# Loading a sample in pieces of eight lines instead of four, in a subject-indexed matrix product with a residual

## The chip, the cores and the metric

The kernel runs on one NeuronCore of a Trainium2 chip; the other cores are idle. The metric is the device time of one execution in microseconds. Before the change it is 326.57 us, the median of three runs (326.31 to 326.69). One further execution was recorded by the hardware profiler; the profile's times are of that one.

## The reference

```python
# x: (128, 128, 1024) float32, subjects: (128,) int32 in 0..7, weights: (8, 128, 128) float32
w = weights[subjects]
out = x + jnp.einsum('bct,bcd->bdt', x, w)
```

For each of 128 samples a 128x128 matrix is chosen by the sample's subject, the sample (128 lines of 1,024 numbers, 512 KB) is multiplied by it, and the sample itself is added. 64 MiB are read and 64 MiB are written.

## The kernel before

All of the weights are loaded once into SBUF (`w_all`). The samples go through SBUF in tiles of four samples (`H * G`, 2 MB): tile `i` lives in slot `i % SLOTS` of twelve buffers `x0` to `x11`, with line `c` of a sample on partition `c`. There are 32 tiles (`NT`). The program is unrolled and its order is written by hand, with one stream of instructions for each engine and semaphores between them.

- SP issues the load of the weights and then all loads of `x`, one DMA for each sample (`load`, called from the loop at line 162). From the thirteenth tile on it first waits until the slot's earlier tile has been stored (lines 165 and 167).
- For each pair of samples (64 of them), POOL waits for the pair's loads and copies the two chosen matrices out of `w_all` (line 196); the index is a register that was loaded from the subjects.
- PE multiplies: four matmuls of 512 columns for a pair's two samples (line 206), into one of two PSUM buffers.
- DVE adds PSUM to the sample and writes the sum over the sample in its slot (line 217).
- ACT issues the store of a tile from the same slot when both pairs are done (`store`, line 223); the first and the last tile are stored in smaller parts.

SP's and ACT's transfers run on two queues over the same 16 DMA engines. A DMA's semaphore rises by one for each of the 16 engines that has finished its share.

`transfer` (line 50) builds the DMA instruction from the two access patterns that it is given. `load` hands it the sample in DRAM regrouped: `ROWS` lines that follow each other in DRAM become one row of the source pattern, and the destination pattern remains 128 partitions of 4 KB each. With `ROWS = 4` the source of a sample is 32 rows of 16 KB, and each goes to four neighbouring partitions. Stores do not use `ROWS`: each partition's 8 KB for two samples is one piece on the SBUF side.

Of the kernel before, what the change touches and what calls it, by code (L numbers as in the profile page):

```python
# [42 lines left out]

IDLE = 3

ROWS = 4
QUEUES = {mybir.EngineType.SP: "qSPDynamicHW", mybir.EngineType.Activation: "qActDynamicHW"}


# [21 lines left out]
def kernel(  # L71
# [49 lines left out]
    def load(engine, i, q):  # L121
# [4 lines left out]
            xs[k][:, q, :],  # L126
            x[i * H * G + q].rearrange("(a r) t -> a (r t)", r=ROWS),
        ).then_inc(s_pair[k][h], DMA)
# [137 lines left out]
```

## Time and profile before

| what | value |
|---|---|
| median of three runs | 326.57 us |
| the profiled execution: its own time | 327.18 us |
| the profiled execution: span from the first to the last instruction | 325.4 us |
| PE busy | 241.1 us (74%) |
| DVE busy | 147.9 us (45%) |
| POOL busy | 34.3 us (11%) |
| read from and written to HBM | 67.63 MB and 67.11 MB |
| mean rate over the span | 414 GB/s |
| loads of `x`: issue to landing, median of 128 | 32.3 us |
| stores of four samples: issue to landing, median of 30 | 47.3 us |
| last load of `x` lands | 271.4 us after the start of the span |

The profile cuts the span into 40 slices and gives for each the busy share of every engine in tenths, the mean busy share of the 16 DMA engines, and the bytes per second. A row for a stretch of time (a window) gives its length, the busy time of PE, of PE's weight loads, of DVE and of POOL with the number of instructions in brackets, the granted TensorE clock, the DMA share and GB/s. A row of waits reads: who waited, at which line, for what; microseconds in total, number of waits, the longest. A queue's row gives its packets, its megabytes and the time of its packets as a share of 16 engines' span.

### The profile page before, as it was taken

How to read it: one execution, taken by the hardware profiler on the slowest of the kernel's cores; microseconds unless marked ns; L12 is line 12 of the kernel's file. 1: busy time of each engine (PE TensorE's matmuls, PEld its weight loads, DVE VectorE, ACT ScalarE, POOL GpSimd, SP SyncE). 2: the span in 40 equal slices, each digit the busy share in tenths (PEclk: the TensorE clock that was granted, in tenths of full speed). 3: DMA queues.
4: the chain of work that ended last, by engine and by line, in shares of the span. 5: the costliest groups of instructions: out<-in, count | busy, mean ns of one | idle time of the engine just before them, and what ended most of it. 6: DMA issues, size and time to landing. Idle time of an engine off the chain costs nothing.

```text
span 325.4 us, 1606 instructions
## 1 busy us (share of the span) xinstructions
PE 241.1 (74%) x518; PEld 95.2 (29%) x518; DVE 147.9 (45%) x68; POOL 34.3 (11%) x132
## 2 busy tenths in 40 slices
PE   6999988988888888888888888888888689000000
PEld 2444332333333333333333333333333233000000
DVE  1375754555555555454555555554554544200000
POOL 1011111011111111111011111111111010000000
PEclk9999999999999999999999999999999889655555
DMA  6999999999999999999999999999999999999994
GB/s 250 413 418 421 428 425 422 420 428 427 426 421 427 429 415 427 424 431 423 423 435 417 416 432 424 428 417 428 433 419 424 418 437 415 429 425 427 426 428 201
DMA packets 16074, 134.85 MB, mean 414 GB/s; under 512 B 2625, under 2 KB 3650, under 8 KB 3906
## 3 DMA queue, kind: packets, MB, share of 16 engines
q1 hardware_dynamic: 7184, 67.64, 49.7%
q10 hardware_dynamic: 8882, 67.11, 49.1%
q8 instruction: 4, 0.07, 0.1%
q14 instruction: 4, 0.03, 0.0%
HBM read 67.63 MB, written 67.11 MB: 414 GB/s over the span
## 4 chain that ended last, share of the span: by engine, by line
PE 42%; DVE 20%; issue 16%; POOL 4%; DMA 2%; POOLq 1%; SPq 0%
PE ps L206 42%; DVE x L217 20%; POOL w L196 4%; DMA x<-in_x_dram 2%; POOLq L196 1%; SPq L57 0%; SPq L161 0%; POOLq L139 0%; SPq L262 0%; SPq L139 0%
## 5 line engine op out<-in xcount | busy, mean ns | idle before, releaser
L206 PE MATMUL ps<-x,w 128*128 128x512 f32 x512 | 236.1, 607 | 33.6 <-POOL w L196 32.1
L217 DVE TENSOR_TENSOR x<-ps,x 128x2048 f32<-128x2048 f32 x64 | 146.7, 2292 | 129.1 <-PE ps L206 129.1
L206 PEld LDWEIGHTS ps<-x,w 128*128 128x128 f32 x512 | 93.3, 191 | 176.6 <-issue 93.9
L196 POOL COPY w<-w_all 128x128 f32 x128 | 34.1, 296 | 238.0 <-DMA x<-in_x_dram 207.7
L146 PE MATMUL ps<-zeros 128*128 128x512 f32 x6 | 5.0, 992 | 1.7 <-DVE zeros L143 1.7
L146 PEld LDWEIGHTS ps<-zeros 128*128 128x128 f32 x6 | 1.8, 328 | 3.7 <-issue 2.1
L143 DVE MEMSET zeros<- 128x512 f32 x1 | 0.5, 485 | 1.1 <-SPq L139 1.1
L153 DVE TENSOR_SCALAR near<-given 1x128 int32<-1x128 int32 x1 | 0.2, 215 | 0.6 <-DMA given<-in_itok_B_dram 0.6
L157 DVE CUSTOM_DVE_ANT_0 index<-near,wrap 1x256 uint16<-1x256 uint16 x1 | 0.3, 278 | 0.0
L155 DVE TENSOR_SCALAR wrap<-near 1x128 int32<-1x128 int32 x1 | 0.2, 216 | 0.0
L253 POOL MEMSET const-float32-0.0<- 128x1 f32 x1 | 0.1, 99 | 0.2 <-issue 0.2
L253 POOL MEMSET const-bfloat16-1.0<- 128x1 bf16 x1 | 0.1, 102 | 0.0
L253 POOL MEMSET const-uint8-127<- 128x1 uint8 x1 | 0.1, 102 | 0.0
L253 POOL MEMSET const-float32-1.0<- 128x1 f32 x1 | 0.1, 99 | 0.0
## 6 DMA issues: line engine op xcount, KB each, us to landing
x<-in_x_dram SPq DMA_DIRECT2D x128, 512.0 KB, 32.3
out_dram<-x ACTq DMA_DIRECT2D x30, 2048.0 KB, 47.3
out_dram<-x ACTq DMA_DIRECT2D x3, 1024.0 KB, 13.9
out_dram<-x ACTq DMA_DIRECT2D x2, 512.0 KB, 21.1
w_all<-in_L_cond_weights_dram SPq DMA_DIRECT2D x1, 512.0 KB, 4.5
given<-in_itok_B_dram ACTq DMA_DIRECT2D x1, 0.5 KB
```

Of the source, the lines that this page charges most:

```text
L143: nc.vector.memset(zeros, 0.0).then_inc(s_zeros, 1)
L146: nc.tensor.matmul(ps[P_SLOTS - 1][:, G - 1, :N], zeros[:, :D], zeros, start=True, stop=True)
L153: nc.vector.tensor_scalar(near, given, -S, S - 1, ALU.max, ALU.min).then_inc(s_index, 1)
L155: nc.vector.tensor_scalar(wrap, near, 0, S, ALU.is_lt, ALU.mult).then_inc(s_index, 1)
L157: nc.vector.tensor_tensor(index, near, wrap, ALU.add).then_inc(s_index, 1)
L196: copy = nc.gpsimd.tensor_copy(ws[b % W_SLOTS], w_all[:, bass.ds(subject[b % R], 1), :])
L206: mm = nc.tensor.matmul(p[:, q % G, t : t + N], ws[(i * H * G + q) % W_SLOTS][:, 0, :], xs[k][:, q, t : t + N], start=True, stop=True,)
L217: nc.vector.tensor_tensor(mine, p, mine, ALU.add).then_inc(s_added, 1)
L253: nc = _bacc.Bacc("TRN2", target_bir_lowering=False, num_devices=1)
```

## The change

One constant is changed. A sample's source pattern becomes 16 rows of 32 KB, and each goes to eight neighbouring partitions; the destination pattern, the number of DMAs, their order, and everything else remain.

```diff
-ROWS = 4
+ROWS = 8
```

It is used in one place:

```python
    def load(engine, i, q):
        k, h = i % SLOTS, q // G
        transfer(
            nc,
            engine,
            xs[k][:, q, :],
            x[i * H * G + q].rearrange("(a r) t -> a (r t)", r=ROWS),
        ).then_inc(s_pair[k][h], DMA)
```

## The prediction

> **What bounds the kernel now.** I began with the slices of the page: a kernel is bound by whatever row never dips.
>
> ```profile
> PE   6999988988888888888888888888888689000000
> DVE  1375754555555555454555555554554544200000
> DMA  6999999999999999999999999999999999999994
> GB/s 250 413 418 421 428 425 422 420 428 427 426 421 427 429 415 427 424 431 423 423 435 417 416 432 424 428 417 428 433 419 424 418 437 415 429 425 427 426 428 201
> ```
>
> The reader is to see that the DMA row is full from the second slice to the last but one, and that the bytes per second stay the same when PE and DVE have nothing left to do (the last five slices). So the transfers set the end, not arithmetic. The queues say how the time of the 16 DMA engines is divided:
>
> ```profile
> DMA packets 16074, 134.85 MB, mean 414 GB/s; under 512 B 2625, under 2 KB 3650, under 8 KB 3906
> ...
> q1 hardware_dynamic: 7184, 67.64, 49.7%
> q10 hardware_dynamic: 8882, 67.11, 49.1%
> ```
>
> q1 is SP's queue (loads), q10 is ACT's (stores); each takes half of the engines' time. Third, the stretches:
>
> ```profile
> 10.00:14.00 4.00, 4.00 (x11) 1.85 (x10) 2.09 (x1) 0.00 (x0) 1.00 1.02 414
> 60.00:100.00 40.00, 34.90 (x76) 13.43 (x75) 21.99 (x10) 5.34 (x20) 1.00 1.01 425
> 276.00:300.00 24.00, 0.35 (x1) 0.00 (x0) 2.29 (x1) 0.00 (x0) 0.56 1.01 427
> 322.00:325.40 3.40, 0.00 (x0) 0.00 (x0) 0.00 (x0) 0.00 (x0) 0.50 0.04 14
> ```
>
> The last column is GB/s: 414 with loads alone, 425 with loads and stores mixed, 427 with stores alone. The waits show what stands behind whom:
>
> ```profile
> POOL w L196 <- DMA x<-in_x_dram: 207.7, 55, 5.6
> DVE x L217 <- PE ps L206: 129.1, 64, 9.0
> ...
> SPq L57 <- DMA out_dram<-x: 78.5, 10, 9.8
> ```
>
> Computation waits for loads (first row), and SP for slots that the stores must empty (last row, in the SP queue's own answer). The DMA engines have work through all of it, so neither wait is on the path.
>
> **The sum of before.** The trace also holds one record for each packet: size, start, duration. A load of one sample is 32 packets of 16 KB (4,096 in all), two for each engine, and 16 four-byte packets that raise the semaphore. A 16 KB load packet lasts 616 ns at the 10th, the 50th and the 90th percentile once stores run, and the next packet of its engine starts 613 ns after it; an 8 KB store packet lasts 311 and is followed after 307; a 4 KB one lasts 159 and is followed after 155. Per engine: 256 load packets by 613 = 156.9 us; 504 stores by 307 = 154.7; 16 short ones by 155 = 2.5; 64 pieces of the weights by 24 ns = 1.5; 164 semaphore packets by 5.5 ns = 0.9. Sum 316.5. The first weights move at 2.1 us and most engines end at 321.4 to 322.2 (the rest of the sum is the start, and the load-only stretch, whose packets last 638 instead of 616); one engine ends at 324.0, and the span at 325.4. That profiled execution took 327.18 us against the median of 326.57, so changes are put onto the median.
>
> **What the change does, part by part.** No instruction is added, removed or moved: 128 issues on SP, 35 stores on ACT, the same waits. Per sample and engine, two packets of 16 KB (four lines each) become one of 32 KB (eight lines); 2,048 load packets go, 128 for each engine.
>
> *Fewer packets.* Two packets of 8 KB cost 2 x 311 - 616 = 6 ns more than one of 16; two of 4 KB cost 2 x 159 - 311 = 7 ns more than one of 8; by the starts instead of the durations the fixed part is 2 x 307 - 613 = 1 ns to 2 x 155 - 307 = 3 ns. So the gain is 128 x 1 to 7 ns, 0.1 to 0.9 us; I take 5 ns, 0.65 us, for removing a boundary inside one queue is what the 4 KB and 8 KB rows measure. It lies on the bound itself, so it counts in full.
>
> *Turns.* An engine alternates between its two queues packet by packet (the records read load, store, load, semaphore, store). Loads get longer turns, stores wait longer, SP reaches its wait for an empty slot earlier. Bytes do not change and both queues have work until 249 us, so I cost it at nothing; its cover is the store backlog (47.3 us from issue to landing on the page, five tiles deep). Were that gone, engines would stand idle for one SP wait, at most 9.8 us.
>
> *Who writes where.* This is the term that decides. Before, an engine's share of a sample is two separate blocks of four lines; after, it must be eight neighbouring lines, because one piece lies on one engine. Which lines an engine gets, and so which part of SBUF it fills at which moment, is dealt anew. The trace has no row in which two engines are known to fill one place at once, so the cost has bounds only. Lower end: none, as 616 ns at all percentiles suggests that an engine is held by itself alone. Upper end: engines in pairs fill the same four-line groups in the same order and halve each other's rate, in step throughout: every 613 ns half of a piece lasts 1,226, so 128 x 2 x 613 = +156.9 us. That loads can hold each other up at all is seen in the load-only stretch: 611 ns undisturbed (10th percentile), 638 at the median, and engines whose packets fell into 641 stay there.
>
> Between the ends it is the lag between the two engines of a pair that counts. Near 100 us the starts of load packets on the sixteen engines lie spread over a whole cycle, so I take lags as evenly spread. The new cycle is 32 KB, store, semaphore, store: 1,226 + 2 x 307 = 1,840 ns. Two halves of 613 overlap by 613 - lag, on average 613 x 613 / 1,840 = 204 ns, and each overlapped ns costs each engine one: 2 x 204 x 128 = +52.3 us for an average pair. But the end is that of the slowest of eight pairs. If lags never changed, the smallest of eight would be about 920 / 9 = 102 ns: 2 x 511 x 128 = +130.8 us. Followed from packet to packet, the lags before hold for some 28 load packets (14 samples) and then jump by 300 to 600 ns, so a pair draws about 128 / 14 = 9 times. One draw (a third of them zero, the rest even from 0 to 613) scatters by 205 ns, the mean of nine by 68, and the worst of eight pairs lies about 1.42 x 68 = 97 above the mean: 204 + 97 = 301 ns, 2 x 301 x 128 = +77 us. I take this, as it uses the row for the lags' life; both ends stay for the range.
>
> [...]
>
> Sum: 326.57 - 0.65 + 77 = 403 us, still with the DMA engines as the bound: PE's 241 us and a chain of 3.7 us for each of 64 pairs of samples stay below it.
>
> **Rivals.**
> 1. *Private streams* (the other side: faster). Each engine's limit is its own, and who writes where is indifferent. For it: the same 307 ns for 8 KB whether one or two queues run. Against it: 638 ns with loads alone. It decides if the load half stays at 613 ns; 326.57 - 0.65 = 325.9 us, from 325.7 to 326.5 by the bounds, half of it within 0.2%.
> 2. *In step.* Lags do not spread, as both engines of a pair receive each sample at the same moment. For it: the first load packets of all engines start within 0.9 us, and store-only engines keep their lags for tens of us. Against it: the spread near 100 us. From +131 to +157 us: 457 to 483 us.
> 3. *Cushioned.* Turns are taken, but data queue in between and a half is only partly blocked. The average pair without the worst-of-eight (+52 us) or less: 335 to 378 us. For it: in the load-only stretch interference is 638 against 611, 4%, not 100%.
> 4. *It does not do what it says.* The transfer's lowering cuts 32 KB back to 16 KB; the trace has no packet above 16 KB. Then 326.6 us.
>
> **How the numbers follow.** Forecast (378 to 455) 0.46; cushioned 0.25; in step 0.13; private streams 0.13; undone 0.03. These chances are a judgement on two rows: interference exists (638), and the only certain gain is 5 ns a packet. Within 0.2% (0.65 us) is what this measurement cannot tell from no change. Private streams go 0.09 to faster and 0.04 to the same, since their gain lies just on that mark; the undone case adds 0.03 to the same. So faster 0.09, same 0.07, slower 0.84. The forecast's own range, cushioned included, is 345 to 455. To leave out no more than the in-step case and a little, the range must reach over the small cases: 325.2 to 455.
>
> **What would show it.** 32 KB load packets in the records, 2,048 fewer in q1. Load packets of 1,226 ns mean private streams; a spread up to 2,452 ns with store packets still at 311 means turns. GB/s of the mixed stretches falls to about 340 for the forecast, and the load-only stretch suffers most. The DMA row stays full: if it shows holes instead, an SP wait for slots has become the bound and my costing of the turns was wrong. The prediction is wrong if GB/s stays at 425.

## The result and the profile after

The changed kernel takes 399.84 us in the median of six runs (383.28 to 415.6), the kernel before 326.49 us beside it (326.3 to 326.69). The ratio is 1.1749 with an interval of 1.1725 to 1.1772; it is formed from the executions near the shortest (383.28 and 383.88), and by the medians it is 1.22, for the changed kernel spreads by 8% from one execution to the next where the six of before lie within 0.4 us. The profiled execution took 383.88 us, with a span of 382.1.

The page of the changed kernel, the rows that answer to those of before (40 slices, then the packets and the two queues):

```profile
PE   5987666686799999986583885839759493900000
DMA  9999999999999999999999999999999999999996
GB/s 220 220 248 281 301 305 295 300 302 316 334 402 421 424 423 425 410 347 356 318 295 366 346 413 314 362 362 352 386 357 411 372 407 357 385 427 426 425 425 281
DMA packets 14026, 134.85 MB, mean 353 GB/s; under 512 B 2625, under 2 KB 3650, under 8 KB 3906
...
q1 hardware_dynamic: 5136, 67.64, 54.7%
q10 hardware_dynamic: 8882, 67.11, 44.6%
```

The DMA engines are still busy from end to end, and the bytes are the same; 2,048 load packets are gone. But a busy engine moves less: the DMA row shows 9 at 220 GB/s as at 425. The rate starts at half of before (220 instead of 413 GB/s), climbs, stands at the full 421 to 425 in slices 13 to 16, falls back to between 295 and 413, and is full again at the end, when stores run alone. A cause that acted evenly, such as a slower packet as such, would not leave whole stretches at full speed (slices 13 to 16).

Windows of the changed kernel (length; PE, PE's weight loads, DVE, POOL with numbers of instructions; clock, DMA share, GB/s):

```profile
18.00:22.00 4.00, 4.00 (x11) 1.82 (x10) 2.86 (x2) 0.53 (x2) 1.00 0.92 213
26.00:100.00 74.00, 53.83 (x115) 21.04 (x114) 32.16 (x15) 7.41 (x28) 0.98 1.00 301
100.00:165.00 65.00, 62.97 (x140) 24.91 (x138) 38.95 (x17) 9.09 (x35) 1.00 1.01 411
165.00:250.00 85.00, 59.31 (x116) 23.49 (x116) 33.69 (x15) 7.85 (x30) 0.90 1.00 346
250.00:340.00 90.00, 60.55 (x118) 24.73 (x116) 35.05 (x16) 7.41 (x28) 0.83 1.01 379
```

The packet records say where the time went. A 32 KB load packet lasts 1,229 ns at the 10th percentile (2 x 616 = 1,232 before), 1,663 at the median, 2,255 at the 99th percentile. What load packets last beyond 1,229 ns and store packets beyond 311 ns, summed and divided by 16 engines, is the cost:

| stretch (us) | median load packet (ns) | excess of loads | excess of stores (us per engine) |
|---|---|---|---|
| start to 26 | 2,252 | 10.2 | 0 |
| 26 to 100 | 1,811 | 16.6 | 4.7 |
| 100 to 165 | 1,231 | 1.7 | 0.5 |
| 165 to 340 | 1,745, then 1,510 | 19.9 | 5.5 |
| all | 1,663 | 48.4 | 10.7 |

48.4 + 10.7 = 59.1 us of excess, less the time saved by longer packets, stands against 382.1 - 325.4 = 56.7 us of span. Nothing else of that size is needed to explain the slowdown; what remained was to find why packets last longer, and why in these stretches.

One more row of waits moved, in the SP queue's own answer, for the changed kernel (who waited, for what: us in total, times, longest):

```profile
SPq L57 <- DMA out_dram<-x: 155.2, 16, 14.3
```

Before it was 78.5 us in 10 waits. What stands behind this row turns out to matter.

### The profile page after: what moved, and what is told of

The parts are those of the page before. It is cut to its first block, busy times and chain, and to the rows that moved or that the text cites. A ratio compares the mean times of both kernels' runs of the same rounds, so it can differ in the third digit from the quotient of the medians.

```text
span 382.1 us, 1606 instructions
## 1 busy us (share of the span) xinstructions
PE 256.4 (67%) x518; PEld 102.4 (27%) x518; DVE 147.8 (39%) x68; POOL 34.0 (9%) x132
## 4 chain that ended last, share of the span: by engine, by line
PE 46%; issue 23%; DVE 13%; POOL 3%; DMA 2%; POOLq 1%; SPq 0%
PE ps L206 46%; DVE x L217 13%; POOL w L196 3%; DMA x<-in_x_dram 2%; POOLq L196 1%; SPq L57 0%; SPq L161 0%; POOLq L185 0%; SPq L262 0%; SPq L139 0%
## 5 line engine op out<-in xcount | busy, mean ns | idle before, releaser
L206 PE MATMUL ps<-x,w 128*128 128x512 f32 x512 | 251.5, 643 | 76.4 <-POOL w L196 72.1
L206 PEld LDWEIGHTS ps<-x,w 128*128 128x128 f32 x512 | 100.5, 205 | 227.5 <-POOL w L196 116.7
## 6 DMA issues: line engine op xcount, KB each, us to landing
out_dram<-x ACTq DMA_DIRECT2D x2, 512.0 KB, 21.3
```

The source lines that it names most:

```text
L206: mm = nc.tensor.matmul(p[:, q % G, t : t + N], ws[(i * H * G + q) % W_SLOTS][:, 0, :], xs[k][:, q, t : t + N], start=True, stop=True,)
```

## The experiments

The changed kernel differs from the one before in three things at once: which partitions an engine fills (the deal, and for one engine its place), how long its packets (and so its turns) are, and at which addresses the 16 engines read DRAM at one moment. The first three runs take them apart. The packet records give queue, size, start and duration, but neither engine nor partition: which engine fills what is inferred from the shapes of the transfers, and an engine's chain is put together from packets that follow each other without a pause.

**E1: the deal of the changed kernel with 16 KB packets.**

```diff
-            xs[k][:, q, :],
-            x[i * H * G + q].rearrange("(a r) t -> a (r t)", r=ROWS),
+            xs[k][:, q : q + 1, :],
+            x[i * H * G + q].rearrange("(a b r) t -> a b (r t)", b=2, r=ROWS),
```

> Packets stay at 16 KB (two per engine and sample, 4,096 in all, as before), but each engine gets eight neighbouring lines, as after the change: the source pattern is written as 16 x 2 rows of 16 KB. If the place that an engine fills decides (two engines whose lines are 32 apart take turns): slow as the changed kernel, 370 to 420 us, and in the load-only stretch (10 to 14 us) about 220 GB/s with packets near 1,126 ns, half of the 2,252 ns of the 32 KB packets. If the size of the piece or the longer turns decide: 326.5 us and 414 GB/s. If reading DRAM at steps of 32 KB from engine to engine decides: slow as well, so this run does not tell that from the place.

That lines 32 apart are one place was an assumption of mine, here as in E3 and E4. The ends of E9 speak for it (partitions 32 to 35: 328.3 us, the next engine 323.7; E7 with 0 to 3: 328.7 and 323.8), its count of long packets does not.

Measured: 344.62 to 351.94 us, median 350.31, beside 326.87. Packets stay at 16 KB (4,096 of them), and in the load-only stretch they last 1,098 ns in the median, about half of 2,252. Windows of this run:

```profile
10.00:14.00 4.00, 3.98 (x5) 1.85 (x6) 0.00 (x0) 0.00 (x0) 0.50 0.99 234
26.00:60.00 34.00, 23.82 (x49) 9.21 (x48) 13.75 (x6) 3.17 (x12) 0.95 1.01 322
60.00:100.00 40.00, 33.50 (x70) 13.07 (x69) 19.76 (x9) 4.77 (x18) 0.96 1.01 389
100.00:165.00 65.00, 56.34 (x123) 21.94 (x122) 35.01 (x16) 7.95 (x30) 1.00 1.01 424
```

So the size of a packet is not what makes the start slow: at 16 KB the rate is 234 GB/s as well. But the total missed what I expected of the place (370 to 420). From 100 us on next to nothing is lost, and it stays so for longer than in the changed kernel: the load packets keep 616 ns up to 270 us, although SP waits nine times for a slot. Then collisions come back here too, as the page shows in the slices from 32 on (second row: SP's waits for a slot in this run):

```profile
GB/s 199 237 242 323 319 328 320 336 371 417 425 428 422 421 425 427 418 421 422 427 425 426 420 424 419 425 426 426 424 422 425 347 370 374 431 423 425 431 423 266
...
SPq L57 <- DMA out_dram<-x: 72.6, 9, 10.8
```

From 270 to 290 us the load packets last 770 ns in the median, and the end costs 2.1 + 1.7 us of excess for loads and stores. Of the change's cost some 23 us come from the deal alone (350.31 against 326.87, medians), and the longer pieces, by their length or by the turns, add the rest.

**E2: the deal of before, DRAM read at steps of 32 KB.**

```diff
-            x[i * H * G + q].rearrange("(a r) t -> a (r t)", r=ROWS),
+            x[min(i * H * G + q, B - 2) : min(i * H * G + q, B - 2) + 2].rearrange(
+                "g (a h r) t -> (g a) h (r t)", h=2, r=ROWS
+            )[:, 0, :],
```

> The deal to partitions of before (two separate groups of four lines per engine, 16 KB packets), but the 32 pieces of 16 KB are read from DRAM at steps of 32 KB, over two neighbouring samples: every second group of four lines is left out and one of the next sample is read in its place, so the output is not the reference's; the amount moved is the same. If the place in SBUF decides: 326.5 us within 1 us, load-only stretch 414 GB/s. If the step in DRAM decides: near the changed kernel, 375 to 415 us.

Measured: 326.75 us, ratio 0.9999 (0.9989 to 1.0009). The windows:

```profile
10.00:14.00 4.00, 4.00 (x10) 1.71 (x9) 1.93 (x1) 0.00 (x0) 1.00 1.03 430
100.00:140.00 40.00, 34.54 (x76) 13.51 (x75) 21.35 (x10) 4.77 (x18) 1.00 1.01 425
```

The two windows after the first have 397 and 393 GB/s where the kernel before had 414 and 418, which is far from the changed kernel's 197 and 213 and doesn't show in the total. So reading at steps of 32 KB does not explain the slowdown, which E1 alone could not say.

**E3: each sample in two halves of 64 lines.**

```diff
-        transfer(
-            nc,
-            engine,
-            xs[k][:, q, :],
-            x[i * H * G + q].rearrange("(a r) t -> a (r t)", r=ROWS),
-        ).then_inc(s_pair[k][h], DMA)
+        for c in (0, C // 2):
+            transfer(
+                nc,
+                engine,
+                xs[k][c : c + C // 2, q, :],
+                x[i * H * G + q, c : c + C // 2].rearrange("(a r) t -> a (r t)", r=ROWS),
+            ).then_inc(s_pair[k][h], DMA)
```

(The counts that are waited for double with it.)

> 16 KB packets read from DRAM at steps of 16 KB, but each sample in two DMAs, lines 0 to 63 and lines 64 to 127; each engine gets one group of four lines of each half, so that two engines always share a place and half of SBUF's lines get nothing at any moment. If the place decides: load-only stretch about 220 GB/s, total 370 to 430 us. If the size of the piece or the step in DRAM decides: 326.5 us plus 128 x 5.5 ns = 0.7 us for twice the semaphore packets, 327.2.

Measured: 337.11 to 349.41 us, median 339.30, ratio 1.0335 (1.0299 to 1.0371). The load-only stretch runs at 250 GB/s with packets of 1,080 ns (before: 414 GB/s and 638 ns), as expected of the place, with packets and DRAM steps as before; the total again misses 370 to 430. Here the collisions end already near 40 us (load packets of 616 ns in the median from 40 us on) and don't return, and SP never waits for a slot at line 57. That the place decides is supported; that its price lasts through the whole kernel is not. Something ends the collisions, and in the changed kernel something brings them back.

**E4: the changed kernel with the engines of a pair set apart at the start.**

```diff
+        for n in (4, 12):
+            transfer(
+                nc,
+                nc.sync,
+                xs[SLOTS - 1][: 4 * n, n // 8, :],
+                x[0, : 4 * n].rearrange("(a r) t -> a (r t)", r=4),
+            ).then_inc(s_stagger[n], DMA)
```

(These stand ahead of the loop over tiles; SP waits for them before it loads that slot.)

> The changed kernel with two small loads in front of the first sample (into a slot that is loaded much later): 16 KB on each of the four lowest engines, then 16 KB on each of the twelve lowest, so that engines 0-3 start the samples one half piece (613 ns) behind 4-7, and 8-11 one behind 12-15. If pairs of engines take turns and the lag between them decides: the load-only stretch goes from 254 and 197 GB/s to 380 or more; the excess of packets over their undisturbed length, about 10 us per engine before 26 us and 21 us from 26 to 100 us, goes in the main, and what comes after SP's first wait for a slot (25 us) stays: 350 to 362 us. If size, turns or DRAM decide: no change from the changed kernel, 383 to 416 us.

Measured: 364.12 to 367.94 us, median 365.82, ratio 1.1208 (1.1166 to 1.1251), for 256 KB more to load. The profiled execution is 20 us shorter than the changed kernel's (364.12 against 383.88), and the longest of E4 is 15 us below the shortest there. It is above the 350 to 362 that I expected. The windows:

```profile
10.00:14.00 4.00, 2.90 (x4) 1.36 (x5) 0.00 (x0) 0.00 (x0) 0.65 0.99 262
26.00:100.00 74.00, 72.71 (x161) 28.64 (x160) 45.78 (x20) 10.68 (x40) 1.00 1.01 419
100.00:165.00 65.00, 54.90 (x119) 21.69 (x118) 34.44 (x16) 8.01 (x30) 0.95 1.01 391
```

From 26 to 100 us the rate is 419 GB/s for 301, and the excess falls from 21.3 to 0.8 + 0.4 = 1.2 us per engine, with the same packets, the same turns and the same deal. Only the moments differ. So here the moments at which the engines start decide the price. The load-only stretch missed by far: 262 GB/s and 1,965 ns instead of 380 GB/s or more. After SP's first emptied queue the losses are those of the changed kernel (21.2 + 5.7 us of excess per engine from 148.6 us, its first gap without loads, to the end).

**E5 and E6: 16 KB store pieces, alone and with the change.** The packet records of the changed kernel show seven gaps of 4.6 to 7.4 us without any new load packet, the first at 172 us; after each, all 16 engines begin a sample together, within 0.3 to 0.5 us. A shorter pause does the same: between 161.7 and 163.3 us only one load packet starts, then 15 start within 0.53 us and last 1,602 to 1,973 ns, where 5 us earlier they lasted 1,231. In E1 it is a pause at 270 us: two load packets start in 0.8 us, then 14 within 0.5 us, and the collisions are back. E6 lengthens the stores' turns so that loads no longer run ahead into the wait for a slot; E5 is its control.

```diff
-            xs[k][:, q0:q1, :].rearrange("d (o g) t -> d o (g t)", g=min(G, q1 - q0)),
+            xs[k][:, q0:q1, :].rearrange("d (o g) t -> d o (g t)", g=q1 - q0),
```

> The changed kernel (32 KB loads) with 16 KB stores: the turns go back towards those of before (load 32, store 16, semaphore, store 16 instead of 32 to 16). If SP's waits for a slot, which the shorter share of the stores brought on, empty the load queue and start the next loads on all engines in step: fewer such waits (before 10, changed 16), few collisions after 165 us (their excess there was 25 us per engine), the early stretch as slow as in the changed kernel: 350 to 365 us. If the late collisions have nothing to do with the turns: 383 to 416 us as the changed kernel.

Measured: 346.53 to 362.45 us, median 356.14. In the SP queue's answer the wait of line 57 has no row any more; these are the longest that are left:

```profile
SPq L139 <- DVEq L139: 44.7, 1, 44.7
SPq L229 <- DMA out_dram<-x: 18.2, 3, 9.7
```

There is no gap between loads above 3 us, and late collisions are gone. The first row is the changed kernel, the others are this run:

```profile
60.00:100.00 40.00, 29.44 (x61) 11.77 (x62) 17.39 (x8) 4.22 (x16) 0.96 1.00 305
26.00:60.00 34.00, 23.90 (x53) 9.05 (x51) 13.75 (x6) 3.18 (x12) 1.00 1.00 316
60.00:100.00 40.00, 28.95 (x64) 11.50 (x64) 18.33 (x8) 4.24 (x16) 1.00 1.00 410
100.00:165.00 65.00, 47.99 (x105) 18.68 (x104) 29.79 (x13) 6.88 (x26) 1.00 1.01 417
165.00:250.00 85.00, 66.03 (x144) 25.57 (x143) 41.24 (x18) 9.53 (x36) 1.00 1.01 420
```

From 165 us to the end the loads' excess is 0.8 + 0.6 = 1.4 us per engine where the changed kernel had 19.9. Up to 60 us this run is about as slow (316 GB/s), but from 60 to 100 us it already has 410 GB/s where the changed kernel had 305, which I had not expected. Of the 59.1 us of excess 22.9 are left: 23 us fewer after 165 us, 11 fewer from 26 to 100 us. So the late part of the cost, from 165 us on, comes by way of the turns; that longer store turns also end the early collisions sooner is seen here, and why is not shown.

> The kernel before with stores read from SBUF in pieces of 16 KB (four samples of a partition) instead of 8 KB; loads stay at 16 KB in the deal of before. No two engines share a place, so only the price of a packet counts: some 4,000 packets go, 250 per engine by 1 to 7 ns, 0.3 to 1.8 us: 324.7 to 326.2, middle 325.2. If longer turns of one queue cost something by themselves: slower than before by 1 us or more.

Measured for E5: 327.54 us, ratio 1.0030 (1.0015 to 1.0044): 0.3% slower, not faster. The price of a packet was right: a 16 KB store lasts 616 ns for 2 x 311, and the packets' sum falls from 321.4 to 320.5 us per engine. But the loads' share of the turns falls too, and the last samples arrive late: the last load packet ends at 313.4 us, before at 271.4. The page of E5:

```profile
PE   5999859667869975778868867778677687686680
GB/s 258 406 417 429 424 428 422 430 423 428 420 424 430 422 426 420 430 426 423 420 430 424 424 422 427 430 422 419 424 432 422 424 424 428 428 424 420 424 370 215
```

PE works up to the last slice but one, where before it stopped in the 34th, and the last but one slice moves 370 GB/s instead of 428: so the end of the kernel now has to wait for late loads and their arithmetic.

**E7 to E10: which partitions are one place.** The kernel before with 12 extra pieces of 16 KB beside the first 12 samples, each on one engine, into partitions `c` to `c + 3` of slots that are loaded later:

```diff
+                if i < 3:
+                    transfer(
+                        nc,
+                        nc.sync,
+                        xs[SLOTS - 3 + i][c : c + ROWS, q, :],
+                        x[0, :ROWS].rearrange("(a r) t -> a (r t)", r=ROWS),
+                    ).then_inc(s_extra, DMA)
```

(SP waits for all twelve before it loads the first of those slots.)

> The kernel before with 12 extra loads of 16 KB beside the first 12 samples, each a single piece (so on one engine), into partitions 0 to 3 of slots that are loaded later: the place that this engine fills anyway. A control for the next: this engine carries three pieces per sample for two, the other fifteen keep packets of 611 to 641 ns until they run out of samples.

> The same 12 extra pieces on the same engine, into partitions 4 to 7: the place of another engine. If a collision holds only the two engines: packets of up to 1,230 ns on two of sixteen engines in the load-only stretch (about one in eight of its packets). If engines that share no place are held too (in the changed kernel's load-only stretch all sixteen ran at the same 2,252 ns): lengthened packets on most engines, where the control has none.

> As the control with the extra pieces on one engine, but into partitions 32 to 35. In the control 3 of 322 load packets that start between 9 and 22 us last 680 ns or longer, with the pieces in partitions 4 to 7 it is 29 of 316. If partitions 0 to 3 and 32 to 35 are one place, filled by this engine anyway: as the control, at most 6. If the place is only the neighbourhood of the partition number: 20 to 35.

> The same into partitions 64 to 67, which by the deal of before another engine fills: 20 to 35 load packets of 680 ns or longer between 9 and 22 us, as with partitions 4 to 7. If only neighbours collide: at most 6.

One execution of each, times from the start of its own span (the counts quoted in the expectations take one start for all runs and differ by one or two):

| pieces into partitions | time (us) | last engine ends (us) | the next one ends | load packets of 680 ns or more, 9 to 22 us |
|---|---|---|---|---|
| 0 to 3 (E7) | 331.79 | 328.7 | 323.8 | 4 of 324 |
| 32 to 35 (E9) | 331.43 | 328.3 | 323.7 | 29 of 297 |
| 4 to 7 (E8) | 335.68 | 332.6 | 325.5 | 29 of 315 |
| 64 to 67 (E10) | 335.15 | 332.1 | 325.9 | 47 of 276 |

By the yardstick that I had set down, the count of long packets, E9 missed: long packets come up there as often as in E8, and why is open. The ends of the packet chains do tell the runs apart: with 0 to 3 and 32 to 35 only the engine with the extra work is late, by the same amount; with 4 to 7 and 64 to 67 that engine ends 4 us later still and a second one about 2 us late, while the other fourteen end by 324.0 us, about as in the control. By the ends, then, 0 to 3 and 32 to 35 are one place for this engine (328.7 and 328.3 us), 4 to 7 and 64 to 67 are others (332.6 and 332.1), and a collision of one pair holds back two engines, not all. The differences of 4 us are well above the 1.2 us by which executions of the kernel before differ, but each rests on one execution, and the count of long packets does not bear out E9.

**E11: a version that might beat both.** 16 KB store pieces only from tile 20 on (`g=(q1 - q0) if i >= 20 else min(G, q1 - q0)`), so that loads keep their turns.

> The kernel before with 16 KB store pieces from tile 20 on only, so that loads keep their share of the turns while they run and the saving of the longer pieces (128 packets per tile for 256, 11 tiles, 88 per engine by 3 to 7 ns) falls into the stretch of stores alone: 0.3 to 0.6 us less than before, 325.9 to 326.2, at the edge of what can be told. If it is the last samples that suffer again as with 16 KB stores throughout: 327 us or more.

Measured: 326.40 us beside 326.77, ratio 0.9990 (0.9981 to 0.9999). The direction is as expected, and the last load packet ends at 275.2 us instead of 313.4, but 0.1% is below what I count as a difference.

## Why the prediction was right, and where it was not

The forecast was 403 us by engines that share a place in SBUF; the median is 399.84 and the range of executions 383 to 416. The mechanism holds: with the deal of before nothing is lost (E2, 326.75 us), with the new deal or with E3's the start is about as slow at 16 KB (234 and 250 GB/s), and the same packets at other moments cost 20 us less in one stretch (E4). The sizes inside the sum were less good than the sum, and that it came within 1% of a median of executions that spread by 8% is luck.

- *Fewer packets*, 0.65 us: an undisturbed 32 KB packet lasts 1,228 ns (E6, median after 165 us) for 2 x 616, 4 ns by 128 = 0.5 us. Right, and of no weight.
- *Turns*, costed at nothing with the store backlog as cover: this step failed. The cover held (the DMA row shows no hole), but I asked only whether engines would idle. Longer load turns let loads reach the wait for a slot sooner and more often (16 waits, 155.2 us); the load queue runs empty, and the next loads start on all engines together, in step. Of the profiled execution's 59.1 us of excess 19.9 + 5.5 = 25.4 come after 165 us; in E6, without those waits, 2 are left. It is the emptied queue and not the wait that counts: E1 waits nine times and pays only from its first pause on, at 270 us. The sign that the prediction gave for this, holes in the DMA row, did not come, as that row counts a held packet as busy (9 in the slices at 220 GB/s, where packets last 2,252 ns).
- *Who writes where*, +77 us from lags that are drawn nine times: the term has the right size in the median (399.84 - 326.49 + 0.5 = 74 us) for a wrong course, and part of that size belongs to the turns. Lags are not drawn evenly. In the load-only stretch nearly the whole price is paid (2,252 ns, near the case of the rival *in step*), later the engines sort themselves out until almost nothing is lost (1,231 ns from 100 to 162 us), and restarts bring the collisions back (1,602 to 1,973 ns after 163.3 us). That sixteen engines meet in eight pairs, on which this term rests, was an assumption of mine that no run shows. What the runs showed in its place is one engine's extra pieces in another's partitions: two engines end late (E8 332.6 and 325.5 us, E10 332.1 and 325.9), the other fourteen by 324.0.
- *Halving*, the upper end of 2,452 ns for a packet: not reached as a pace. In the load-only stretch packets last 2,252 ns. If the two engines of a pair overlap there in full, they move 2 x 32,768 bytes in that time, 29.1 GB/s, against 26.7 for one alone (16,384 bytes in 613 ns); if they overlap in part only, the place may be no faster than for one. The records do not tell these apart.
- *Stores at 311 ns*: wrong, stores are held up too. 1,287 store packets last over 320 ns, 442 in the mean, and carry 10.7 of the 59.1 us.
- *The rivals*: private streams are excluded by E4, where the same packets of the same deal last less at other moments; the transfer was not cut back (2,048 packets of 32 KB); in step describes the start, and cushioned no stretch.
- *The mixed rate*, about 340 GB/s: 301, 411, 346 and 379 in the four windows.

## What to carry to other kernels

The shape of a DMA's outer dimension changed which engine fills which partitions: as the runs read, 32 rows of four lines gave each engine a place of its own (load packets of 616 ns at the median), 16 rows of eight did not (1,663 ns, undisturbed 1,229), and on this kernel, which is bound by its transfers, this cost 17% (22% by the medians), where the longer packet brought 0.5 us. Look at the shortest and the median packet of a queue, not at the DMA busy row, which here shows 9 at 220 GB/s as at 425. And when a turn between two queues is lengthened, ask what the favoured queue will run into: here waits for a buffer emptied it (seven gaps of 4.6 to 7.4 us), and after each gap all engines set going within 0.3 to 0.5 us.

## What the runs showed of the hardware that I had not expected

In the load-only stretch of the changed kernel all sixteen engines keep one pace, 2,245 to 2,259 ns a packet, though their starts lie spread over 1.4 us; with the engines set apart (E4) nine packets in ten last 1,950 ns or more, and half of all 1,960 to 1,968. If the pairs were independent, I would expect different lags to give different paces. E8 speaks against a general jam, for there only two engines ended late (332.6 and 325.5 us, the other fourteen by 324.0). What ties the engines together there stays open, and with it why the stretch in E4 was not faster (262 GB/s).

Engines that take turns with stores sort themselves out: after 100 us in the changed kernel (until its first pause) and in E1 (until 270 us), after some 40 us in E3, collisions nearly vanish (packets of 1,231, 616 and 616 ns) although nothing in the program spaces the engines. How they find these lags was not tried.

A four-byte semaphore packet takes a turn of its own between the two queues: load, store, semaphore, store is the order in the records of the changed kernel. So 32 KB loads and 8 KB stores share the engines 32 to 16 in bytes, where 16 KB loads (load, store, load, store, semaphore, store; the prediction lists one store too few) had 32 to 24. From 100 to 140 us the bytes moved stand 2.1 to 1 and 1.4 to 1.
